# Sixteen-head attention: the divided output multiplied on GpSimd and turned back later, with another opening and another table of places

## The chip, the cores and the metric

The kernel runs on one core of one Trainium2 chip. The metric is the device time of one execution in microseconds (us). Each time given for a kernel is the median of several runs; every profile is of one execution. In the profile the engines are PE (TensorE matmuls), PEld (its weight loads), DVE (VectorE), ACT (ScalarE), POOL (GpSimd) and SP (SyncE, here a queue of DMAs).

## What is computed

A two-layer decoder on x of shape (8, 256, 256), all in float32. Layer 0 adds three results in turn to x: self-attention with 16 heads of width 16, cross-attention of 16 heads over a given context with a key bias and a mask by length, and a feed-forward part in which 8 experts each choose 32 tokens of a batch after a Sinkhorn balancing. Layer 1 adds causal self-attention (16 heads of width 16), a second cross-attention with 16 heads of width 64, and another feed-forward part with routed experts. The change lies in the three attentions with heads of 16:

```python
q, k, v = heads(x @ Wq.T + bq), heads(x @ Wk.T + bk), heads(x @ Wv.T + bv)
q, k = rope(q), rope(k)
attn = softmax(q @ k.T / 4)            # layer 1: causal
out = (attn @ v).merge_heads() @ Wo.T + bo
x = x + out
```

## The kernel before

**Units and steps.** The three attentions are 24 units that run one after the other, one batch each: four times (two self-attentions of layer 0, then two cross-attentions), units 0 to 15, and then eight causal self-attentions of layer 1, units 16 to 23. Each unit has four steps k = 0 to 3. A step is one group of eight heads (c, the half of the width of 256) and one half of the keys (kt); so steps 0 and 1 are group 0, and steps 2 and 3 are group 1.

**A step on the engines.** `scores` (L326) makes the products of keys and queries on PE (`st`, L334), then two exponentials on ACT (`pT`, L345) and, in layer 1, two masking selects on POOL (L350). `values` (L362) multiplies the weights by the values on PE (`o`, L371); the values have a column of ones beside them, so that the sums of the weights come out too. The program issues the scores of the next step ahead of the values of this one. The score tile has one buffer (pool `scp`, L567), so the scores of a step wait until both exponentials of the step before have read it. The output tile `o` has one buffer as well.

**The division.** At the end of a group (odd k) `values` calls `divided_T` (L382): DVE turns `o` in blocks of 32x32 so that queries lie on partitions (`by_q`, L387), takes reciprocals of the sums (`dens`, L389), multiplies (`att`, L391) and turns the result back (`attT`, L397). All four are DVE instructions, one behind the other. There are 48 such groups.

**What stands beside the steps.** The order of every engine is the order in which the code emits instructions (`manual_schedule` over five engines). Work of other units and of the experts is emitted between the steps by a table: `beside(n, k, at, piece)` (L850) puts a piece at step k of unit n, in the order of `at`. Pieces with `at` EARLY (0) come ahead of the values of the step, the others behind them (`run`, L853). A self-attention unit is prepared by such pieces: `stats` and `norm` (L434, L437: layer norm; the power on POOL, L258; the rows on POOL, L262, except in the first two units), `rows` (L444: transposes `tr` on PE), `heads(0)` and `heads(1)` (L452: the product `qk` on PE, three rotary multiplications on DVE, one or two additions on POOL), `joined` (L462: the last addition, on DVE), `vals` (L465), `begin` (L470: the transposes of keys and queries and the masked queries `qm` on ACT). `out(t)` (L486) is the output product of one half of the rows (`ao`) and its addition to x on DVE (L492); it stands in two places, one for each half t. A cross-attention unit's `out` (L552) turns the result back on PE (`oR`) and adds it.

**The experts of layer 0** are the generator `chosen_experts` (L633), one for each pair of batches. It yields 27 times, and four lists, `pieces` (used for the first two pairs), `sooner` and `soonest`, give for each yield its place relative to the unit at which that pair is done. In order the yields are: statistics and norm of the two batches (`xnb`, POOL L262); transposes of each (`tr <- xnb`); the gate product `lg` of each; eight rounds of balancing (`cs`, `rc`, `g`); four rounds of picking the top values, the last of which writes the chosen slots to memory and reads them back by three DMAs (L688 to L694); then one that turns the slots into columns (`cps` on PE, L698, `col`) and makes the first selection matrix (`pick`, POOL L709); and for each batch the gathering product `rps`, the expert product `y` (with `put` on POOL L738 and `ys` on DVE L756), and the scattering product `back`, which is added to x (L765).

**The opening** (the code behind the lists): unit 0 is normed, its heads, values and `joined` are emitted, then unit 1 is normed, unit 0 begins, its first scores are emitted, and only then come the rows and the first heads of unit 1.

**Behind the units** come tables for the second cross-attention (`tables_x`, L807; product `nvw`, L839), that cross-attention (from about 470 us on in the profile) and the last feed-forward part. The change does not touch them.

Of the kernel before, what the change touches and what calls it, by code (L numbers as in the profile page):

```python
# [29 lines left out]
F32 = mybir.dt.float32  # L30
# [4 lines left out]
ALU = mybir.AluOpType  # L35
# [4 lines left out]
P = 128  # L40
B, S, D = 8, 256, 256
# [116 lines left out]
def plain(  # L158
# [121 lines left out]
    def product4(out, lhsT, rhs, start, stop):  # L280
        for h in range(0, P, HP):
            nc.tensor.matmul(  # L282
                out[h : h + HP], lhsT[:, h : h + HP], rhs, start=start, stop=stop, skip_group_check=True
            )
# [31 lines left out]
    class Core:  # L316
# [9 lines left out]
        def scores(self, step):  # L326
# [32 lines left out]
                pTs.append(pT)  # L359
            self.exps[step] = pTs  # L360

        def values(self, step):  # L362


            c, kt, q0 = self.queries(step)
            if kt == 0:
                self.o = op.tile([P, 2, S], F32, tag="o", name="o")
            o, pTs = self.o, self.exps.pop(step)
            for m in range(2):
                for j in range(4):  # L370
                    nc.tensor.matmul(  # L371
                        o[HP * j : HP * j + HP, m, q0:],
                        self.v_pad[:, kt, 8 * c + 2 * j + m, :],
                        pTs[j // 2][:, j % 2, m, : S - q0],
                        start=kt == 0 and m == 0,
                        stop=kt == 1,
                        skip_group_check=True,
                    )
            if kt:
                divided_T(self.attT[:, c, :], o, self.dens[:, c, :])  # L380

    def divided_T(dst, o, r):  # L382


        n = S // HP
        by_q = work.tile([P, 2, n, HP], F32, tag="by_q", name="by_q")
        nc.vector.transpose(by_q.rearrange("p m n w -> p (m n w)"), o.rearrange("p m q -> p (m q)"))  # L387
        r = r.rearrange("p (m n) -> p m n", m=2)
        nc.vector.reciprocal(r, by_q[:, :, :, HD])  # L389
        both = work.tile([P, n, 2, HD], F32, tag="both", name="att")  # L390
        nc.vector.tensor_tensor(  # L391
            both.rearrange("p n m d -> p m n d"),
            by_q[:, :, :, :HD],
            r.unsqueeze(3).to_broadcast([P, 2, n, HD]),
            ALU.mult,
        )
        nc.vector.transpose(dst, both.rearrange("p n m d -> p (n m d)"))  # L397

    def rotary(qk, t, layer, work):
# [26 lines left out]
    class SelfAttention:  # L426
# [10 lines left out]
        def norm(self):  # L437
            self.xn = work.tile([P, 2, D], F32, tag="xn", name="xn")
            for t in range(2):
                self.head = normed(  # L440
                    self.xn[:, t, :], x[:, 2 * self.b + t, :], self.mv, self.rs, t, nc.gpsimd if self.n else nc.vector
                )

        def rows(self):  # L444
# [38 lines left out]
                    xt = x[:, 2 * self.b + t, :]  # L483
                    nc.gpsimd.tensor_tensor(xt, xt, self.bias[1], ALU.add)

        def out(self, t):  # L486
            b, attT = self.b, self.core.attT
            xt = x[:, 2 * b + t, :]
            ps = mm.tile([P, 2 * D], F32, tag="mm", name="ao")[:, :D]
            for c in range(2):  # L490
                product4(ps, attT[:, c, bass.ts(t, P)], self.wo[:, c, :], c == 0, c == 1)
            nc.vector.tensor_tensor(xt, xt, ps, ALU.add)  # L492

# [78 lines left out]
    def turn():  # L574
        for t in range(2):
            qc, qs = rotary(bs[:, :2, :].rearrange("p i d -> p (i d)"), t, 0, work)
            nc.vector.tensor_tensor(turned[:, t, :], qc, qs, ALU.add)
# [272 lines left out]
    def beside(n, k, at, *made):  # L850
        plan.setdefault((n, k), []).append((at, made))

    def run(n, k, early):  # L853
        for at, made in sorted(plan.get((n, k), ()), key=lambda p: p[0]):
            if (at == EARLY) == early:
                for one_made in made:
                    one_made()

    EARLY = 0
    for n, u in enumerate(units):  # L860
        if u.__class__ is SelfAttention:
            u.n = n
            if n in (20, 22):
                beside(n - 2, 0, 80, u.stats)
                beside(n - 2, 1, EARLY, u.norm)
            else:
                beside(n - 3, 2, 80, u.stats)
                beside(n - 3, 3, EARLY, u.norm)
            beside(n - 2, 2, 30, u.rows)
            beside(n - 2, 3, 30, partial(u.heads, 0))  # L870
            beside(n - 1, 0, 30, partial(u.heads, 1))
            beside(n - 1, 1, EARLY, u.joined)
            beside(n - 1, *((2, 30) if u.layer == 0 and n % 4 else (1, 30)), partial(u.vals, 0))
            beside(n - 1, 1, 60, u.begin)
            beside(*((n, 0, 40) if u.layer else (n - 1, 2, 31) if n % 4 else (n - 1, 3, 40)), partial(u.vals, 1))
            beside(n, 3, 80, u.biased)
            for t in range(2):
                beside(n + 1, *((2 + t, 40) if u.layer else (0, 20 + t)), partial(u.out, t))
        else:
            beside(n - 1, 0, 80, u.stats, u.vals)  # L880
            beside(n - 1, 1, EARLY, u.norm)
            beside(n - 1, 1, 60, u.begin)
            beside(n + 1, *((2, 40) if n % 4 == 2 else (0, 20)), u.out)
    beside(0, 2, 40, add_up)
    beside(2, 2, 85, slot_keys)
    beside(3, 2, 50, slot_tables)

    begun = (-1, 2, 80), (0, 0, EARLY), (0, 1, 80)
    start = begun + (
        (0, 2, EARLY), (0, 3, 40), (0, 3, 41), (1, 0, 70), (1, 2, 70),  # L890
        (1, 3, 70), (2, 0, 15), (2, 1, 5), (2, 2, 10), (2, 2, 70), (2, 3, 70), (3, 0, 70), (3, 1, 45),
        (3, 2, 70), (3, 3, 85),
    )
    pieces = start + (
        (4, 1, 85), (4, 2, EARLY), (4, 3, 70), (5, 1, 10), (5, 2, 10), (5, 3, 10), (5, 3, 20), (6, 1, 10), (6, 2, 15),
    )
    sooner = start + (
        (4, 1, 84), (4, 1, 85), (4, 3, 20), (5, 0, 50), (5, 1, 35), (5, 2, 20), (5, 2, 50), (5, 3, 50), (6, 0, 50),
    )
    soonest = begun[:2] + (  # L900
        (0, 0, 80), (0, 1, EARLY), (0, 1, 65), (0, 1, 66), (0, 2, 50), (0, 2, 51),
        (0, 3, 60), (1, 0, 45), (1, 1, 10), (1, 1, 70), (1, 2, 70), (1, 3, 35), (1, 3, 70), (2, 0, 35),
        (2, 0, 70), (2, 1, 85), (2, 2, EARLY), (2, 2, 85),
        (3, 0, 10), (3, 0, 50), (3, 1, 35), (3, 2, 35), (3, 2, 50), (3, 3, 35), (4, 0, 50),
    )
    ex = [chosen_experts(2 * i, 2) for i in range(B // 2)]
    for i, made in enumerate(ex):
        for n, k, at in (pieces, pieces, sooner, soonest)[i]:
            beside(4 * i + 4 + n, k, at, partial(next, made, None))

    for u in units[:2]:
        u.n = 0
        u.stats()
        u.norm()
        if u is units[0]:
            opening = ExitStack()
            opening.enter_context(tc.issue_after(u.head.ins))
            order = ExitStack()
            order.enter_context(tc.manual_schedule(engines=PINNED))
            turn()  # L920
            u.rows()
            u.heads(0)
            u.vals(0)
            u.heads(1)
            u.joined()
            u.vals(1)
            for v in units[:2]:
                v.load()
        else:
            units[0].begin()  # L930
            units[0].core.scores(0)
            u.rows()
            u.heads(0)
            key_tables()
    for n, u in enumerate(units):
        if n == 1:
            expert_tables()
# [22 lines left out]
                wd, ctxs, wproj, wkv_x, wq_x, wout_x, nkrow, nvcol, lns, lnb = weights_x()  # L960
        opening.close()
    order.close()
    for t in range(2):
        units[-1].out(t)
    wn, nvw, hot8 = tables_x(wd, wq_x, wout_x, nkrow, nvcol)
    first.close()
    banks.close()
# [1880 lines left out]
```

## Time and profile before

| what | value |
| --- | --- |
| three runs | 1214.85, 1215.27 and 1216.22 us, median 1215.27 us |
| the profiled execution | 1214.46 us |
| its span, from the first to the last instruction | 1212.7 us |
| PE busy in the span | 1141.0 us (94%) |
| PE busy from 0 to 470 us, the part with the 24 units | 413.04 of 470 us (16.91 of the first 30, 396.13 of the next 440) |
| PE busy from 470 us to the end | 727.99 of 742.70 us |
| DVE, ACT and POOL busy from 30 to 470 us | 288.17, 236.47 and 209.76 of 440 us |

The page lists busy time by engine, then by groups of instructions: line of the code, engine, operation, the tile written and the tiles read, shapes, count; behind a bar the busy time and the mean duration of one in ns; behind the next bar the idle time of that engine just ahead of those instructions and what ended it. In a list in order of time the columns are start (us), duration (us), engine, line, operation, tiles, shape, count, and in brackets the idle time of the engine ahead of it with the instruction that ended it. Matmul durations are pipelined, so a sum of them is more than their busy time.

### The profile page before, as it was taken

The page shows a single profiled execution, that of the slowest core. Times are in us where ns is not written, and L with a number is a line of the kernel's source. Part 1 is how long each engine was busy: PE and PEld are TensorE (multiplying, and loading weights), DVE is VectorE, ACT ScalarE, POOL GpSimd, SP SyncE. Part 2 cuts the span into 40 slices and gives each one's busy share as a digit, 9 for nine tenths or more (in the row PEclk, how much of TensorE's full clock was granted, in tenths as well). Part 3 has the DMA queues.
Part 4 walks back from the last instruction along what each step waited for, and adds up shares of the span by engine and source line. Part 5 has one row for each costly group of instructions (what it writes and reads, how often), then busy time and mean ns, then how long its engine had stood idle before and what let it go on. Part 6 is the DMA issues. An engine that isn't in the chain of part 4 may idle for free.

```text
span 1212.7 us, 31559 instructions
## 1 busy us (share of the span) xinstructions
PE 1141.0 (94%) x13596; PEld 707.9 (58%) x13596; DVE 562.4 (46%) x1564; ACT 447.6 (37%) x696; POOL 417.2 (34%) x482
## 2 busy tenths in 40 slices
PE   5798989998999998999999999999999999999997
PEld 2344435444444445566666676666666486888874
DVE  4455767758775746223332433333335474222113
ACT  2666655656434361223232323232323131222220
POOL 2335344443746741132333323241416105000004
PEclk9999999999999999999999999999999999999999
DMA  7036232050200410010101010101012108599934
GB/s 223 1 127 205 91 117 91 2 171 2 83 2 11 167 71 2 18 37 18 37 19 37 18 37 19 37 19 37 19 37 72 36 2 322 217 399 404 386 123 138
DMA packets 51446, 116.76 MB, mean 96 GB/s; under 512 B 8273, under 2 KB 36417, under 8 KB 46945
## 3 DMA queue, kind: packets, MB, share of 16 engines
q1 hardware_dynamic: 45120, 98.90, 23.9%
q0 software_dynamic: 3456, 12.73, 2.9%
q10 hardware_dynamic: 2720, 3.02, 0.7%
q8 instruction: 109, 1.79, 0.6%
q14 instruction: 41, 0.33, 0.1%
HBM read 104.00 MB, written 27.93 MB: 109 GB/s over the span
## 4 chain that ended last, share of the span: by engine, by line
PE 73%; POOL 8%; DVE 7%; issue 6%; ACT 3%; DMA 2%; SPq 0%; POOLq 0%; ACTq 0%; DVEq 0%
PE h L276 7%; PE k L276 6%; PE v L276 6%; PE wo L276 5%; PE ox L1458 5%; PE stx L1419 4%; PE out L1836 4%; PE out L1653 3%; PE st L334 3%; PE h L1041 3%; PE o L371 3%; PE qk L282 3%; PE q L276 3%; PE tr L291 2%; PE fm L276 2%
## 5 line engine op out<-in xcount | busy, mean ns | idle before, releaser
L345 ACT ACTIVATE pT<-st 128x1024 f32<-128x1024 f32 (+1 forms) x128 | 110.5, 917 | 79.3 <-PE st L334 79.1
L371 PE MATMUL o<-pT,padv 128*32 128x256 f32 (+1 forms) x1536 | 100.4, 372 | 4.3 <-POOL pT L350 4.2
L1425 POOL TENSOR_TENSOR both<-pTx 128x512 f32<-128x512 f32 x64 | 82.1, 1310 | 50.5 <-issue 44.9
L371 PEld LDWEIGHTS o<-pT,padv 128*32 128x32 f32 x1536 | 40.9, 110 | 87.4 <-issue 41.7
L276 PE MATMUL h<-xrT,w 128*64 128x128 f32 (+1 forms) x1936 | 87.3, 250 | 3.1 <-issue 3.1
L276 PEld LDWEIGHTS h<-xrT,w 128*64 128x64 f32 x1936 | 84.7, 137 | 6.1 <-issue 3.9
L258 POOL TENSOR_TENSOR lnrs<-lnve,mhalf 128x2 f32<-128x2 f32 x48 | 35.1, 732 | 153.2 <-DVE lnve L256 141.8
L345 ACT ACTIVATE pT<-st,kbias 128x1024 f32<-128x1024 f32 x64 | 67.8, 1112 | 36.7 <-PE st L334 36.7
L1423 ACT ACTIVATE pTx<-stx 128x1024 f32<-128x1024 f32 x64 | 62.2, 1022 | 41.3 <-PE stx L1419 26.2
L1034 DVE TENSOR_TENSOR midr<-sl,h 128x128 f32<-128x128 f32 x102 | 29.4, 288 | 102.5 <-PE h L276 68.9
L334 PE MATMUL st<-qm,kT 32*128 32x512 f32 (+1 forms) x512 | 68.7, 606 | 5.2 <-ACT pT L345 3.3
L1033 ACT ACTIVATE sl<-h 128x128 f32<-128x128 f32 (+1 forms) x114 | 35.3, 310 | 97.8 <-PE h L276 58.8
L1419 PE MATMUL stx<-qTx,kTx 64*128 64x256 f32 x512 | 64.3, 391 | 2.5 <-ACT pTx L1423 2.5
L282 PE MATMUL qk<-l_wqkv,xnT 128*32 128x512 f32 x512 | 63.9, 616 | 2.2 <-ACT xnT L294 2.2
L1458 PE MATMUL ox<-pTx,vx 128*64 128x256 f32 x512 | 62.3, 385 | 0.0
L1513 POOL TENSOR_TENSOR oT<-oT,rs 128x512 f32<-128x512 f32 x30 | 37.3, 1274 | 66.7 <-DMA rs<-rd 66.7
L258 POOL TENSOR_TENSOR lxrs<-lxve,mhalf 128x2 f32<-128x2 f32 x8 | 5.6, 702 | 154.3 <-DVE sc L1172 123.3
L1419 PEld LDWEIGHTS stx<-qTx,kTx 64*128 64x128 f32 x512 | 46.1, 186 | 20.3 <-ACT pTx L1423 7.2
L276 PE MATMUL wo<-wout_x,oT 128*64 128x256 f32 x512 | 58.0, 379 | 0.0
L350 POOL TENSOR_SCALAR_AFFINE_SELECT pT<-pT 128x512 f32<-128x512 f32 x64 | 42.1, 671 | 39.3 <-ACT pT L345 39.3
L1458 PEld LDWEIGHTS ox<-pTx,vx 128*64 128x64 f32 x512 | 33.9, 136 | 26.4 <-issue 12.1
L1466 DVE COPY oT<-ox 128x512 f32<-128x512 f32 x16 | 11.1, 691 | 81.0 <-PE ox L1458 81.0
(361 smaller groups left out, 2195.1 us busy)
## 6 DMA issues: line engine op xcount, KB each, us to landing
w<-packs SPq DMA_DIRECT2D x22, 1408.0 KB
w<-packs SPq DMA_DIRECT2D x22, 768.0 KB
rs<-rd SPq DMA_DIRECT2D x16, 512.0 KB
packs<-L_ffn_w_eDF SPq DMA_DIRECT2D x8, 704.0 KB
packs<-L_ffn_w_eDF SPq DMA_DIRECT2D x8, 640.0 KB
packs<-L_ffn_w_eFD SPq DMA_DIRECT2D x8, 640.0 KB
ctxT<-ctx_T SPq DMA_DIRECT2D x8, 512.0 KB
wkv_x<-L_xattn_Wkv POOLq DMA_DIRECT2D x1, 4096.0 KB, 14.0
```

The source lines that it names most:

```text
L258: nc.gpsimd.tensor_tensor(rs[:, :n], ve[:, :n], mhalf[:, :n], ALU.pow)
L276: nc.tensor.matmul(out[h], lhsT[:, h], rhs, start=start, stop=stop, skip_group_check=True)
L282: nc.tensor.matmul(out[h : h + HP], lhsT[:, h : h + HP], rhs, start=start, stop=stop, skip_group_check=True)
L334: nc.tensor.matmul(st[:, r, :, :n], self.kT[rows, c, bass.ts(kt, P)], self.qm[rows, :, c, q0:], start=True, stop=True,)
L345: nc.scalar.activation(pT[:, :, :, :n], st[:, 2 * k : 2 * k + 2, :, :n], AF.Exp, scale=self.scale, **kb)
L350: nc.gpsimd.affine_select(out=pT[:, :, :, :P], in_=pT[:, :, :, :P], compare_op=ALU.is_ge, fill=0.0, base=0, pattern=[[0, 2], [0, 2], [1, P ...
L371: nc.tensor.matmul(o[HP * j : HP * j + HP, m, q0:], self.v_pad[:, kt, 8 * c + 2 * j + m, :], pTs[j // 2][:, j % 2, m, : S - q0], start=kt ...
L1419: nc.tensor.matmul(st[:, g, kt, :], kT[rows, c, bass.ts(kt, P)], qT[rows, c, :], start=True, stop=True)
L1423: nc.scalar.activation(pT, st, AF.Exp, scale=scale)
L1425: nc.gpsimd.tensor_tensor(both, pT[:, :, 0, :], pT[:, :, 1, :], ALU.add)
L1458: nc.tensor.matmul(o[XD * g : XD * (g + 1), i, :], v[:, kt, 2 * (c2 + i) + g, :], pT[:, g, kt, :], start=kt == 0, stop=kt == 1, skip_group ...
L1836: nc.tensor.matmul(ps[h], mid[:, i, h], sets[k % len(sets)][1][:, i, :], start=i == 0, stop=i == NFC - 1, skip_group_check=True,)
```

## The change

The diff has five parts.

1. **The division is split.** `divided` keeps the first turn and the reciprocals on DVE, and its multiplication is issued on GpSimd. The turn back is a function of its own (`turned_back`), which a new piece calls at place 84 of steps 1 and 3 of every unit, behind nearly all that stands beside these steps.
2. **The output product of a self-attention unit is one piece**: both halves of the rows into one PSUM tile and one addition to x with 512 elements, at the place where the first half stood (in layer 1 step 2 at 40; the second half stood in step 3).
3. **Other places**: `rows` in layer 1 at 60 instead of 30; a cross-attention's `out` in front of a self-attention at 40 instead of 20; and in the lists of the experts the second yield one step later, the yield with `cps` and `pick` one piece or one step later, the last `back` of the first two pairs one step later, and several in `sooner` and `soonest`.
4. **The norms of units 20 and 22 on DVE** instead of GpSimd.
5. **The opening**: the norm, the rows and the first heads of unit 1 are emitted ahead of the second values, the begin and the first scores of unit 0.

```diff
+        def turn(self, c):
+            turned_back(self.attT[:, c, :], self.both)
...
             if kt:
-                divided_T(self.attT[:, c, :], o, self.dens[:, c, :])
-
-    def divided_T(dst, o, r):
+                self.both = divided(o, self.dens[:, c, :])
+
+    def divided(o, r):
...
-        nc.vector.tensor_tensor(
+        nc.gpsimd.tensor_tensor(
             both.rearrange("p n m d -> p m n d"),
             by_q[:, :, :, :HD],
             r.unsqueeze(3).to_broadcast([P, 2, n, HD]),
             ALU.mult,
         )
+        return both
+
+    def turned_back(dst, both):
         nc.vector.transpose(dst, both.rearrange("p n m d -> p (n m d)"))
...
-                    self.xn[:, t, :], x[:, 2 * self.b + t, :], self.mv, self.rs, t, nc.gpsimd if self.n else nc.vector
+                    self.xn[:, t, :], x[:, 2 * self.b + t, :], self.mv, self.rs, t, nc.gpsimd if self.n not in (0, 1, 20, 22) else nc.vector
...
-        def out(self, t):
-            b, attT = self.b, self.core.attT
-            xt = x[:, 2 * b + t, :]
-            ps = mm.tile([P, 2 * D], F32, tag="mm", name="ao")[:, :D]
-            for c in range(2):
-                product4(ps, attT[:, c, bass.ts(t, P)], self.wo[:, c, :], c == 0, c == 1)
-            nc.vector.tensor_tensor(xt, xt, ps, ALU.add)
+        def out(self):
+            attT, xb = self.core.attT, x[:, 2 * self.b : 2 * self.b + 2, :]
+            ps = mm.tile([P, 2, D], F32, tag="mm", name="ao")
+            for t in range(2):
+                for c in range(2):
+                    product4(ps[:, t, :], attT[:, c, bass.ts(t, P)], self.wo[:, c, :], c == 0, c == 1)
+            nc.vector.tensor_tensor(xb, xb, ps, ALU.add)
...
-            beside(n - 2, 2, 30, u.rows)
+            beside(n - 2, 2, 60 if u.layer else 30, u.rows)
...
-            for t in range(2):
-                beside(n + 1, *((2 + t, 40) if u.layer else (0, 20 + t)), partial(u.out, t))
+            beside(n + 1, *((2, 40) if u.layer else (0, 20)), u.out)
...
-            beside(n + 1, *((2, 40) if n % 4 == 2 else (0, 20)), u.out)
+            beside(n + 1, *((2, 40) if n % 4 == 2 else (0, 40)), u.out)
+    for n, u in enumerate(units):
+        beside(n, 1, 84, partial(turned_again, u, 0))
+        beside(n, 3, 84, partial(turned_again, u, 1))
...
-    begun = (-1, 2, 80), (0, 0, EARLY), (0, 1, 80)
+    begun = (-1, 2, 80), (0, 1, EARLY), (0, 1, 80)
...
-        (4, 1, 85), (4, 2, EARLY), (4, 3, 70), (5, 1, 10), (5, 2, 10), (5, 3, 10), (5, 3, 20), (6, 1, 10), (6, 2, 15),
+        (4, 1, 85), (4, 2, EARLY), (5, 0, 60), (5, 1, 10), (5, 2, 10), (5, 3, 10), (5, 3, 20), (6, 1, 10), (6, 3, 10),
...
-        (4, 1, 84), (4, 1, 85), (4, 3, 20), (5, 0, 50), (5, 1, 35), (5, 2, 20), (5, 2, 50), (5, 3, 50), (6, 0, 50),
+        (4, 1, 84), (4, 1, 85), (5, 0, 20), (5, 0, 50), (5, 1, 35), (5, 2, 50), (5, 3, 10), (5, 3, 60), (6, 0, 50),
...
-    soonest = begun[:2] + (
-        (0, 0, 80), (0, 1, EARLY), (0, 1, 65), (0, 1, 66), (0, 2, 50), (0, 2, 51),
-        (0, 3, 60), (1, 0, 45), (1, 1, 10), (1, 1, 70), (1, 2, 70), (1, 3, 35), (1, 3, 70), (2, 0, 35),
+    soonest = (-1, 2, 80), (0, 0, EARLY), (0, 0, 80), (0, 1, EARLY)
+    soonest += (
+        (0, 2, 35), (0, 2, 36), (0, 3, 10), (0, 3, 50),
+        (1, 0, 10), (1, 0, 70), (1, 1, 35), (1, 1, 70), (1, 2, 70), (1, 3, 35), (1, 3, 70), (2, 0, 35),
         (2, 0, 70), (2, 1, 85), (2, 2, EARLY), (2, 2, 85),
-        (3, 0, 10), (3, 0, 50), (3, 1, 35), (3, 2, 35), (3, 2, 50), (3, 3, 35), (4, 0, 50),
+        (3, 0, 70), (3, 1, 50), (3, 2, 35), (3, 3, 10), (3, 3, 35), (4, 0, 10), (4, 0, 50),
     )
...
-    for u in units[:2]:
-        u.n = 0
-        u.stats()
-        u.norm()
-        if u is units[0]:
...
-            turn()
-            u.rows()
-            u.heads(0)
-            u.vals(0)
-            u.heads(1)
-            u.joined()
-            u.vals(1)
-            for v in units[:2]:
-                v.load()
-        else:
-            units[0].begin()
-            units[0].core.scores(0)
-            u.rows()
-            u.heads(0)
-            key_tables()
+    first_u, second_u = units[:2]
+    first_u.stats()
+    first_u.norm()
...
+    turn()
+    first_u.rows()
+    first_u.heads(0)
+    first_u.vals(0)
+    first_u.heads(1)
+    first_u.joined()
+    second_u.stats()
+    second_u.norm()
+    second_u.rows()
+    first_u.vals(1)
+    first_u.begin()
+    second_u.heads(0)
+    first_u.core.scores(0)
+    key_tables()
...
-    for t in range(2):
-        units[-1].out(t)
+    units[-1].out()
```

`turned_again(u, c)` calls `u.core.turn(c)`. The calls of `load` that the opening loses did nothing for these two units (L430).

## The prediction

> **What bounds the kernel now.** I read the busy times first: PE works 1141.0 of 1212.7 us, and from 470 us to the end 727.99 of 742.70 us. The change touches nothing there, so that part only moves. In the 470 us before it PE works 413.04 us; 57 us are waits, and they are all that a new order can win. The second view lists for what PE waited up to 470 us (total, times, longest, in us):
>
> ```profile
> engine line waited for: us in total, times, longest us
> PE st L334 <- ACT pT L345: 8.5, 8, 1.5
> PE tr L291 <- DVE xn L262: 7.9, 1, 7.9
> PE tr L291 <- DVE qkr L463: 7.8, 7, 1.7
> PE cps L698 <- DMA by_half<-slots: 6.8, 3, 2.9
> PE qpsx L547 <- DVE xnx L262: 4.3, 4, 1.1
> PE o L371 <- POOL pT L350: 4.2, 5, 1.6
> PE back L282 <- DVE ys L756: 3.0, 2, 1.5
> PE tr L291 <- POOL xnb L262: 2.3, 2, 1.5
> ```
>
> No single engine binds; PE stops where a piece stands too early in its queue. The third view, PE in order of time, shows what such a stop costs, and the fourth the clock behind it (busy times by engine, then granted clock, DMA share, GB/s):
>
> ```profile
> 168.34 1.09 PE L291 MATMUL tr<-ident,xnb 128*128 128x128 f32 x8
> 171.60 0.32 PE L698 MATMUL cps<-ident,by_half 4*128 4x4 f32 x2 [2.16 <-DMA by_half<-slots]
> 171.73 2.10 PE L334 MATMUL st<-qm,kT 32*128 32x512 f32 x8
> 173.76 1.68 PE L371 MATMUL o<-pT,padv 128*32 128x256 f32 x16
> ```
> ```profile
> 171.60:175.20 3.60, 3.60 (x26) 1.37 (x30) 0.17 (x1) 1.22 (x2) 2.44 (x3) 0.53 1.03 339
> ```
>
> The reader is to see that `st` elsewhere takes 1.14 us and here 2.10, because after a wait of 2.16 us the clock was 0.53 for 3.6 us. So this wait cost 2.16 + 0.47 x 3.6 = 3.9 us. The one at 246.19 us (2.92 us, then 0.57 for 3.5 us) cost 4.4.
>
> The Trainium skill ("TensorE: Matmul & The Clock Gate", section "What's actually happening") says that the clock halves after an idle window of about 3.4 us. By that rule alone neither wait would have slowed PE, and the forecast would be about 3 us higher; the measured 0.53 decides.
>
> **What goes.** Each place was followed through the compiled order of the changed kernel, with durations of this trace.
> - *`cps` later.* It now stands behind the next scores, values and `ao` (first two pairs) or behind `qk` and `v` (the fourth). First pair: `tr <- xnb` ends at 169.43, the exponentials free the score tile at 169.5, `st` to 170.6, `o` to 171.6, `ao` to 173.4, `cps` (its DMA is long there) and `lg` to 174.1; the next `st` starts at 174.15 instead of 177.38: 3.2 us. Second pair by the same steps 4.4 us. Fourth pair 1.68 us at 375.38. **9.3 us.**
> - *The second yield later.* At 98.02, 161.67 and 235.51 PE waits 0.57, 1.36 and 1.34 us for `qkr` of DVE, which waits for `qc` on POOL, which stands behind two rows of `xnb` (2.42 us). These rows now stand behind `qc`: **3.3 us.** What is next late there, `tr <- qkr`, has its input 0.3 us early by my count.
> - *The last `back` of the first two pairs later.* It waited 1.48 us twice (204.13, 278.80). The step it leaves has 3.0 us of PE work, less than the 3.44 us from one `st` to the next that the exponentials allow (56.04 to 59.48), so 0.4 us of each comes back: **2.1 us.**
> - *`tr <- xnb` of the fourth pair later:* waits of 1.49 and 0.77 us, of which 0.7 comes back, since the last row of `xnb` still ends at 316.7: **1.6 us.**
> - *Units 20 and 22 normed on DVE.* Before, the selects, `xn` on POOL (2.42 us) and the waits around 365 and 411 us cost 1.4 us each. After, DVE waits for the power (`lnrs`, to 362.53) and takes 0.73 us, then `by_q` follows late, and `o` with its single buffer waits 0.6 us: 0.85 twice, **1.7 us.**
>
> Together **18.0 us**.
>
> **What comes.**
> - *The opening.* PE now has unit 1's transposes in front of unit 0's second values. Their input is ready at 21.9 us as before (DVE's order is the same), so PE stands from 16.41 to 21.9, where it had four short waits. From there: transposes, values (at a slow clock, as behind other long waits), `begin`, `qk`, and the first `st` at about 27.9 instead of 21.76 us; but `qk` and the transposes are then done, and the fourth `st` comes at 38.8 instead of 36.85: **2.0 us** lost, from 0 to 4 by how long the clock stays down.
> - *One addition of 512 for two of 256.* Two take 0.42 each, of which the second starts after `ao`; one takes 0.69 (the row of `x<-x,oR`). Where PE then waits for `xnx` (4 times) it waits 0.27 longer: **1.1 us.** The two halves of `ao` in one step of layer 1 are PE work either way; in the last two units, with little else beside them, the chain comes out 0.1 us later.
> - *The product on GpSimd.* The operation isn't in the trace. The nearest rows:
>
> ```profile
> L391 DVE TENSOR_TENSOR att<-by_q,dens 128x256 f32<-128x256 f32 x48 | 22.0, 458 | 1.6
> L484 POOL TENSOR_TENSOR x<-x,offset 128x256 f32<-128x256 f32 x16 | 11.5, 738 | 7.1 <-DVE offset L585 7.1
> L459 POOL TENSOR_TENSOR qkr<-qc,qs 128x512 f32<-128x512 f32 x16 | 20.6, 1284 | 4.3 <-DVE qs L418 3.7
> ```
>
> I take 0.74 us, POOL's own row of as many elements and inputs; the ends are 0.40 (POOL's copy of 128x256 in pieces of 16, L307) and 1.28 (twice the elements). DVE loses 48 x 0.46 = 22 us, POOL gains 48 x 0.74 = 36 us on 210 of 440 us busy. Neither total is a bound; places are. In layer 0 the turn back comes late enough: unit 0's ended at 45.87 and `ao` started at 46.93; product and hand-over add 0.45 us, so 0.6 us is left, and the cover in the other units is like it (0.2 to 1 us). In 28 of 48 groups other DVE work stands between the reciprocals and the turn back; in the other 20 DVE waits about 0.9 us for POOL, with `stats` or an addition behind it. In layer 1 each of 16 products stands in front of the next selects. It starts 1.1 us after `o` ends and takes 0.74; the next first select can start 1.5 us after `o` at the earliest, so the delay is at most 0.35 us, less with filler on PE: 0 to 5.6 us, taken at the middle, **2.8 us.**
> - *Two engines on one memory path.* DVE's `g` (0.19 us) took 1.21 us while POOL added two tensors:
>
> ```profile
> 348.57 1.28 POOL L459 TENSOR_TENSOR qkr<-qc,qs 128x512 f32<-128x512 f32 x1 [1.16 <-DVE qs L418]
> 348.69 1.21 DVE L662 TENSOR_TENSOR g<-g,rc 128x32 f32<-128x32 f32 x1
> ```
>
> With 36 us more of such work on POOL, DVE's additions of two SBUF tensors will be held more often; most have cover of a step. 0 to 4 us, taken at **1.0.**
>
> The Trainium skill ("GPSIMD Engine Reference", section "Engine selection") speaks against this move: two-input elementwise work belongs on VectorE, GpSimd being about twice as slow. The rows agree in kind (738 against 458 ns, 1.6 times); by twice the DVE row the product would take 0.92 us and the layer-1 delay grow by up to 0.18 x 16 = 2.9 us, so about 1207 us.
>
> **The sum.** 18.0 - 2.0 - 1.1 - 0.1 - 2.8 - 1.0 = 11.0 us less. Against the profiled execution's own 1214.46 us (span 1212.7, with 1.76 around it) that is 1203.5; the median of the three runs lies 0.8 us above that execution, so I forecast **1204.3 us**.
>
> **Rivals.**
> - *Wider gain.* DVE, relieved of two instructions in front of the rotary products, hands `qkr` over earlier (waits of 0.93 and 0.43 us at 362 and 408), and the products hide wholly: 11.0 + 2.8 + 1.0 + 1.0, so about 1199.5. For it: the selects had waits of 4.2 us only.
> - *Half is given back.* PE arrives earlier than POOL's `pick` (1.83 us), `put` (1.9) and rows behind it; the five won places turn into waits for these, as the 1.62 us of `o` for the selects at 303 us do now. Half of 18.0 kept: 9.0 - 7.0 = 2 to 5 us, about 1211.
> - *Slower: the selects behind the product.* The product is far slower than my row, or waits long for the reciprocals behind other DVE work, and POOL, which takes its queue in order, holds the masking selects of layer 1. The 16 places must lose 13.8 us (the 11.0 and the 2.8 I already gave) before the change loses, 0.86 us each: a product that ends 1.2 us after the select could start. With 1.2 us of loss each: 1204.3 - 2.8 + 19.2, about 1221. Against it: in the trace POOL's two-input rows hardly vary (716 to 902 ns for L484).
> - *Nothing to measure.* The opening costs its 4 us, the lock its 4, the selects their 5.6, and the wins are 15: about 1215.
>
> **Chances.** The forecast, 1201.5 to 1208: 0.42. Wider gain, 1196 to 1201.5: 0.16. Half, 1208 to 1212.8: 0.19. Nothing, 1212.8 to 1217.7, which is within 0.2%, about what a measurement of this kernel can tell from no change: 0.08. Slower: 0.15. So faster 0.77, same 0.08, slower 0.15. The range is 1197 to 1216; it leaves out the slow rival and the last microsecond of the wide gain.
>
> **What would show it.** In the list of PE's waits: `cps <- by_half` and `back <- ys` gone, `tr <- qkr` down from 7.8 to about 4 us, `tr <- xnb` under 1; one wait of about 5.4 us at 16 us; the clock near 1.0 at 172 and 246 us; `att` on POOL near 740 ns; `o <- pT` from 4.2 to at most 10 us. The start of `fm <- ctxT` (from 471.6 us) should be 11 us earlier, and all behind it unchanged. I am wrong if `o <- pT` grows past 15 us, if `att` takes over 1.2 us, if the opening costs over 4 us, or if new waits for `pick`, `put` or `attT` stand where `cps` and `back` stood.

## The result, and the profile after

The changed kernel takes 1215.33 us (median of 12 runs, 1211.78 to 1217.58), the kernel before 1215.74 us beside it (12 runs, 1208.77 to 1219.43). The ratio is 1.0001, with a 95% interval from 0.9987 to 1.0016: no difference that can be measured, where I forecast 11 us less. The profiled execution took 1217.2 us, so it is one of its longer ones.

The first matmul behind the 24 units (`fm <- ctxT`, first in each fence below from the lists of PE in order of time; changed kernel first, then before) shows that the part that the change touches ended 2.2 us later in this execution, and not 11 us earlier:

```profile
473.78 0.65 PE L276 MATMUL fm<-ctxT,wkv_x 128*64 128x256 f32 x2
```
```profile
471.59 0.65 PE L276 MATMUL fm<-ctxT,wkv_x 128*64 128x256 f32 x2
```

PE's waits from 0 to 470 us in the changed kernel, in the same columns as the prediction's list:

```profile
engine line waited for: us in total, times, longest us
PE tr L291 <- DVE xn L262: 13.0, 2, 7.5
PE st L334 <- ACT pT L345: 10.7, 8, 2.1
PE cs L282 <- DVE g L674: 8.8, 6, 2.7
PE qpsx L553 <- DVE xnx L262: 5.7, 4, 1.5
PE o L374 <- POOL pT L350: 4.3, 6, 1.6
PE ao L282 <- DVE attT L403: 3.2, 1, 3.2
PE o L374 <- DVE by_q L390: 2.6, 3, 1.2
PE tr L291 <- DVE qkr L469: 2.2, 3, 0.9
PE rps L282 <- POOL pick L715: 1.9, 2, 1.7
...
PE tr L291 <- POOL xnb L262: 0.6, 1, 0.6
PE cps L704 <- DMA by_half<-slots: 0.2, 1, 0.2
```

Nearly every wait that I struck out is gone: `cps` from 6.8 to 0.2 us, `tr <- xnb` from 2.3 to 0.6, `tr <- qkr` from 7.8 to 2.2, and `back <- ys` (3.0) is not in the list. The selects, which I feared, cost what they did (4.3 for 4.2). But `cs <- g`, 1.1 us before and no line of my forecast, stands at 8.8 us, and the last `ao <- attT` went from 2.2 to 3.2. The clock is whole where the wait for `cps` stood, as forecast (stretch; busy times of PE, its weight loads, DVE, ACT and POOL, each with its number of instructions; granted clock, DMA share, GB/s):

```profile
171.40:174.80 3.40, 3.40 (x78) 1.85 (x78) 0.53 (x2) 2.04 (x3) 2.29 (x4) 1.00 0.76 240
```

So the question is not whether the gains came, but what took them back.

**A measure for small steps.** The runs of one kernel spread over some 6 us (the changed kernel) to 11 us (the one before). But the order on each engine is fixed, and apart from stretches of half clock (granted clock 0.50 in the profile), and what waits behind them, a step takes the same time to 0.1 us in every kernel whose order there is the same. So besides ratios I compare the start of each step's scores (`st`, in the list of PE in order of time). Changed kernel less before, in us, at the start of units 1, 9, 10, 13, 14, 16, 17, 19 and 23: +1.5, +1.1, -2.4, -1.7, -6.0, -3.7, -6.3, +4.7, +2.7. The two `cps` places show as -3.5 (in unit 9) and -4.3 (in unit 13). Then come losses that I did not forecast: +3.3 in unit 11, +3.3 in unit 15, +11 in units 17 and 18. Steps show one execution, with its own stretches of half clock: the profiled one of the changed kernel has nine up to 470 us, that of before five, and three of the nine lie between units 17 and 19. The changed kernel with `back` put back, whose order is the same there, had none there and took 3.5 us less from the start of unit 17 to that of 20; so part of the 11 us is chance.

### The profile page after: what moved, and what is told of

Read it like the earlier page. It is cut to its first block, busy times and chain, and to the rows that moved or that the text cites. A ratio compares the mean times of both kernels' runs of the same rounds, so it can differ in the third digit from the quotient of the medians.

```text
span 1215.4 us, 31522 instructions
## 1 busy us (share of the span) xinstructions
PE 1143.1 (94%) x13596; PEld 711.9 (59%) x13596; DVE 546.2 (45%) x1504; ACT 447.7 (37%) x696; POOL 440.6 (36%) x526
## 4 chain that ended last, share of the span: by engine, by line
PE 74%; POOL 8%; issue 6%; DVE 5%; ACT 4%; DMA 2%; SPq 0%; POOLq 0%; ACTq 0%; DVEq 0%
PE h L276 7%; PE k L276 5%; PE v L276 5%; PE ox L1466 5%; PE st L334 5%; PE wo L276 4%; PE stx L1427 4%; PE o L374 4%; PE out L1844 4%; PE out L1661 3%; PE qk L282 3%; PE h L1049 3%; PE q L276 3%; ACT pT L345 2%; PE tr L291 2%
## 5 line engine op out<-in xcount | busy, mean ns | idle before, releaser
L276 PEld LDWEIGHTS wo<-wout_x,oT 128*64 128x64 f32 x512 | 36.8, 137 | 18.5
```

The lines of the kernel that those rows point to most:

```text
L276: nc.tensor.matmul(out[h], lhsT[:, h], rhs, start=start, stop=stop, skip_group_check=True)
```

## The experiments

Four batches ran, each on another chip and beside the kernel before, which took 1219.9, 1219.8, 1216.6 and 1220.0 us in them; so each kernel is told by its ratio to before in its own batch. Gains and losses in us are that ratio times before's time, and "by steps" means differences of the starts of `st`.

**First batch: one part at a time.**

```diff
-    begun = (-1, 2, 80), (0, 0, EARLY), (0, 1, 80)
+    begun = (-1, 2, 80), (0, 1, EARLY), (0, 1, 80)
...
-        (4, 1, 85), (4, 2, EARLY), (4, 3, 70), (5, 1, 10), ...
+        (4, 1, 85), (4, 2, EARLY), (5, 0, 60), (5, 1, 10), ...
```

> The kernel before with three numbers of its tables changed: the second yield of the experts one step later for the first three pairs, and the yield with cps and pick one piece of the step later for the first two pairs. Nothing else of the change. Theory A (the gains of the moved places are real, and others of the change gave them back): the two cps places gain 3.5 and 4.3 us as the profile of the changed kernel shows at units 9 and 13, the second yield up to 1.4 us in each of three places, so 7 to 11 us less than before: 1205 to 1209 us. Rival B (the places gain only together with the relief of DVE, since pick, put and the rows behind cps come late in any case): less than 4 us gained, 1212 to 1216 us.

Ratio 0.9924 (0.9902 to 0.9946): 9.3 us less. By steps 3.5 us in unit 9 and 4.3 in unit 13 for `cps`, and 0.1, 0.9 and 0.9 for the second yield of the three pairs, 9.7 in all. At `fm` the difference is 10.0 (461.59 against 471.59): a stretch of half clock more in unit 16 took 1.5 us, and one less near 465 us gave it back. Theory A: two changed entries of the tables ("the three moved numbers" below) win nearly what the whole change was to win.

```diff
-    ... (5, 3, 10), (5, 3, 20), (6, 1, 10), (6, 3, 10),
+    ... (5, 3, 10), (5, 3, 20), (6, 1, 10), (6, 2, 15),
```

> The changed kernel with one place undone: the last back of the first two pairs again in step 2 instead of step 3. Theory A (the wait at back was a wait for DVE's queue; with back gone the next cs stands there and waits longer, 2.69 us at 203 and at 274 us, with half the clock behind it): the two cs waits go, the two back waits of about 1.5 us return, half the clock behind them goes: 2.4 us less at each of the two places, about 1210.5 us against 1215.3 for the changed kernel. Rival B (the moved back was worth the 2.1 us that I forecast, and the loss is elsewhere): 1217 us.

Ratio 0.9951 (0.9937 to 0.9965): 6.0 us less than before, and the changed kernel with `back` moved is level with before (1.0001, in the first comparison). By steps 2.1 us at unit 10 to 12 and 2.6 at 14 to 16: theory A. The list of PE in order of time of the changed kernel shows why:

```profile
198.74 1.07 PE L374 MATMUL o<-pT,padv 128*32 128x256 f32 x16
199.62 0.29 PE L282 MATMUL cs<-g,ones 128*32 128x16 f32 x16
199.85 0.66 PE L291 MATMUL tr<-ident,xn 128*128 128x128 f32 x4
203.19 0.32 PE L282 MATMUL cs<-g,ones 128*32 128x16 f32 x16 [2.69 <-DVE g L674]
203.44 2.09 PE L334 MATMUL st<-qm,memk 32*128 32x512 f32 x8
205.46 1.70 PE L374 MATMUL o<-pT,padv 128*32 128x256 f32 x16
206.99 1.90 PE L282 MATMUL back<-ys,put 128*32 128x256 f32 x32
```

and DVE at the same time:

```profile
199.27 0.48 DVE L745 SCALAR_TENSOR_TENSOR junk<-idx_row,col,later 128x256 f32<-128x256 f32 x1
...
200.88 0.88 DVE L762 TENSOR_SCALAR ys<-y,weight 128x256 f32<-128x256 f32 x2
201.67 0.43 DVE L403 STREAM_TRANSPOSE attT<-att 128x256 f32<-128x256 f32 x1
202.03 0.22 DVE L667 RECIPROCAL rc<-cs 128x16 f32<-128x16 f32 x1
...
202.95 0.19 DVE L674 TENSOR_TENSOR g<-g,rr 128x32 f32<-128x32 f32 x1
```

With `back` put back (same list, this experiment):

```profile
200.75 0.29 PE L282 MATMUL cs<-g,ones 128*32 128x16 f32 x16
202.64 1.93 PE L282 MATMUL back<-ys,put 128*32 128x256 f32 x32 [1.60 <-DVE ys L762]
204.50 0.66 PE L291 MATMUL tr<-ident,xn 128*128 128x128 f32 x4
205.09 0.32 PE L282 MATMUL cs<-g,ones 128*32 128x16 f32 x16
205.34 1.14 PE L334 MATMUL st<-qm,memk 32*128 32x512 f32 x8
```

The reader is to see DVE, not PE. Between the first `cs` and the next one DVE has `junk`, `weight`, `ys`, the turn back and a whole round of balancing, 3.9 us without a pause. The next `cs` needs the last of it. `back` waited 1.6 us in the middle of that chain, and its own 1.93 us covered the rest. Taken out of there, it leaves the chain as long as it was and PE with nothing but 0.66 us of `tr`; it waits 2.69 us at the end of the chain in place of 1.6 in the middle, and does `back` in the next step besides. From one `cs` to the next it is then 3.57 us in place of 4.34, so that step gets 0.8 us shorter; the next gets 3.3 us longer, by `back` itself and by the half clock behind the wait (`st` 2.09 us for 1.14).

```diff
-        nc.gpsimd.tensor_tensor(
+        nc.vector.tensor_tensor(
             both.rearrange("p n m d -> p m n d"),
```

> The changed kernel with the division's product back on DVE, the turn back still at its late place. Theory A (the product is not what the gains were lost to; PE's waits for the selects are 4.3 us in the changed kernel and 4.2 before): within 2 us of the changed kernel, 1213 to 1217 us. Rival B (the hand-over to GpSimd and back, and two engines on one memory path, are what was lost): 4 to 8 us less, 1207 to 1211 us.

Ratio 0.9970 (0.9956 to 0.9984): 3.7 us less, between the two theories. The steps tell more: against the changed kernel nothing changes from unit 1 to unit 16 (0.5 us later at unit 1, 0.7 at unit 16), and 3.8 us are won from the start of unit 16 to that of 23, one stretch of half clock among them. So the product's price is paid in layer 1.

The fourth kernel has the opening of the diff's fifth part, and nothing else of the change.

> The kernel before with the new opening alone. Theory A (the opening costs what the steps of the first units show, 1.5 us at unit 1 and 3.0 at unit 3): 1.5 to 3 us more than before, 1217 to 1219 us. Rival B (cross-attention, where the exponentials set the pace, takes it back): within 1 us of before.

Ratio 1.0019 (1.0006 to 1.0032): 2.3 us more. By steps 2.3 us, from unit 1 unchanged to unit 9; behind it, where the order is that of before, other stretches of half clock make it 2.5 to 4.2. Theory A.

**Second batch: one more part each, on the kernel with the three moved numbers** (0.9924).

The lists `sooner` and `soonest` of the diff:

> The kernel before with the three moved numbers for the first pairs of batches (9.3 us less than before, measured) and the lists of the third and fourth pair of the changed kernel. Theory A (my forecast: the fourth pair's cps 1.7 and tr for xnb 1.6 are gains of their own): about 3.3 us less than without the lists, 12.6 us less than before. Rival B (in layer 1 the new places put other waits where the old ones stood: rps for pick 1.65 us at 326 us and cs for g 1.67 at 352 us of the changed kernel, each with half the clock behind it): 2 to 5 us more than without the lists, 4 to 7 us less than before.

Ratio 0.9906 (0.9881 to 0.9930), 11.5 us less than before; by steps 3.2 us less at unit 23 than without the lists (the ratios' intervals overlap). Theory A by the steps, though new waits for `pick` (1.16 us) and `ys` (1.51) do appear in unit 17.

```diff
-                    ... self.rs, t, nc.gpsimd if self.n else nc.vector
+                    ... self.rs, t, nc.vector if self.n in (0, 20, 22) else nc.gpsimd
```

> The kernel before with the three moved numbers and the norms of units 20 and 22 on DVE. Theory A (my forecast): the waits of tr for xn around 365 and 411 us go, 0.85 us each after what by_q costs: 1.7 us less than without, 11 us less than before. Rival B (o waits 1.17 us for by_q in both places, as in the changed kernel): within 0.7 us of the kernel without it in the places of units 19 to 22.

Ratio 0.9942 (0.9918 to 0.9966), 7.1 us less than before, so no gain on 0.9924; by steps 1.2 us are lost by unit 23. PE's `o` waits 1.17, 0.54 and 1.17 us for `by_q` where `tr` had waited 0.77 twice. Theory A fell, and so did rival B: from unit 19 to 23 2.7 us are lost. Most of it stands at the `cps` of unit 19, which waits 2.52 us in place of 1.68, with half clock behind it.

The split division, its product on GpSimd and the turn back at place 84 of the table, as in the diff's first part:

> The kernel before with the three moved numbers, the division's product on GpSimd and the turn back at its late place. Theory A (my forecast): nothing in layer 0, 2.8 us for the selects and 1.0 for the shared memory path in layer 1, so 3.8 us more than without it, 5.5 us less than before. Rival B (the product and its hand-over are hidden wherever the lists of the experts are the old ones): within 1 us of the kernel without it.

Ratio 1.0008 (0.9984 to 1.0032): the 9.3 us are gone. Both theories missed. By steps layer 0 loses nothing, and units 16 to 19 lose some 11 us: `oR` waits 2.17 us for the turn back at 297 us, `cps` 3.94 us for its DMA at 316 and 2.57 at 375. The trace shows how the late product delays the first of these DMAs (columns as before; SPq issues DMAs):

```profile
303.84 0.26 DVE L392 RECIPROCAL dens<-by_q 128x16 f32<-128x16 f32 x1
304.94 2.42 POOL L262 TENSOR_SCALAR xnb<-x,lnmv,lnrs 128x256 f32<-128x256 f32 x2
307.34 0.61 POOL L394 TENSOR_TENSOR att<-by_q,dens 128x256 f32<-128x256 f32 x1
307.98 0.45 DVE L403 STREAM_TRANSPOSE attT<-att 128x256 f32<-128x256 f32 x1 [3.89 <-POOL att L394]
310.96 0.33 SPq L694 DMA_DIRECT2D slots<-top  x1
```

The product's inputs are ready at 304.1 us, but POOL has two selects and two rows of `xnb` in front of it. DVE stands 3.89 us for the turn back, and the picking of the top values, which ends in those DMAs, stands behind the turn back in DVE's queue. With the three numbers alone the same DMA is issued at 307.03 us. So the price depends on what the lists put in front of the product on POOL and behind the turn back on DVE; no run moved those rows alone.

The output product in one piece, with one addition, as in the diff's second part:

> The kernel before with the three moved numbers and the output product of a self-attention unit in one piece with one addition. Theory A (my forecast): PE waits 0.27 us longer for xnx in four places and 0.1 us at the end, 1.2 us more than without it. Rival B (the four places are hidden behind the exponentials, and one addition less frees DVE): no difference of 0.5 us.

Ratio 1.0023 (0.9998 to 1.0048): 12 us more than without it, against 1.2 in theory A. By steps 0.3 to 0.4 us in each of the four places of layer 0, as forecast, and once more in unit 11; 2.1 us in unit 15, where half clock came up; and 6.6 us in layer 1.

**Third batch: parts of the changed kernel undone in turn, and the merged output product taken apart.**

```diff
-            beside(n + 1, *((2, 40) if u.layer else (0, 20)), u.out)
+            for t in range(2):
+                beside(n + 1, *((2 + t, 40) if u.layer else (0, 20 + t)), partial(u.out, t))
```

> The changed kernel with one part undone: the output product of a self-attention unit again in two halves with an addition each, in the two places of before. The changed kernel takes as long as the one before (ratio 1.0001). Theory A (the merged output product took back most of the gain, as it did by some 9 us on the other base): 5 to 9 us less than before. Rival B (there it was an accident of that base's lists, and the changed kernel's table fits the merged one): within 2 us of before.

Ratio 0.9927 (0.9907 to 0.9947): 8.9 us less than before. Theory A.

The same with the last `back` in step 2:

> The changed kernel with two parts undone: the output product in two halves, and the last back of the first two pairs in step 2 as before. Theory A (the losses are separate and add up: 6 us for back, 5 to 9 for the output product): 11 to 15 us less than before. Rival B (the two share DVE's queue, so that one undone does most of it): 6 to 9 us less than before.

Ratio 0.9925 (0.9906 to 0.9943): 9.1 us less than before, at the upper end of rival B and below theory A. By steps `back` gives 0.5 us at unit 11 and 2.6 at unit 15; the last section shows where the other 2 went.

The same with the product on DVE:

> The changed kernel with three parts undone: the output product, the last back, and the product of the division on DVE again (the turn back at its late place). What is left of the change is the new opening, the lists, the norms on DVE, and the late turn. Theory A (the product costs some 3.5 us in layer 1 with these lists): 3.5 us less than with the product on GpSimd, 14 to 18 us less than before. Rival B (with the output product in two halves the product on GpSimd is hidden): within 1 us of the kernel with two parts undone.

Ratio 0.9861 (0.9839 to 0.9883): 16.9 us less than before (16.6 between the medians). By steps the product's move is worth 0.5 us in layer 0 and 2.8 in layer 1. Theory A. Between the ratios it is 7.8 us, over twice the steps; the two profiled executions are the fastest of the one kernel and the slowest of the other, and which figure is nearer is not settled.

The fourth starts from the three moved numbers:

```diff
-                beside(n + 1, *((2 + t, 40) if u.layer else (0, 20 + t)), partial(u.out, t))
+                beside(n + 1, *((2, 40 + t) if u.layer else (0, 20 + t)), partial(u.out, t))
```

> The kernel before with the three moved numbers, and in layer 1 the second half of the output product moved from step 3 to step 2, straight behind the first; still two tiles and two additions. It parts the place from the single addition. Theory A (the place costs: step 3 and the wait at the end lose the work that filled them, step 2 gets late): most of the 6.6 us that the merged output product lost in layer 1, 4 to 7 us more than with the three numbers alone. Rival B (the single long addition costs, as my forecast had it): within 1 us of the three numbers alone.

Ratio 0.9963 (0.9950 to 0.9976): 4.8 us more than with the three numbers alone; by steps 7.6 us from unit 17 to 23, where the merged one lost 6.7, each with one to two stretches of half clock more than the three numbers alone. Theory A: in layer 1 it is the place, not the long addition. (In layer 0, where the place did not move, the 4 us that the merged one lost are the addition's and the half clock's.) PE in unit 18, first with the half in step 3 (the three numbers alone), then with both halves in step 2:

```profile
338.45 0.29 PE L282 MATMUL cs<-g,ones 128*32 128x16 f32 x16
338.57 1.05 PE L282 MATMUL ao<-l_wo,attT 128*32 128x256 f32 x16
340.33 1.97 PE L727 MATMUL y<-experts,rT 128*32 128x256 f32 x32 [0.71 <-DVE qs L418]
342.40 0.32 PE L282 MATMUL cs<-g,ones 128*32 128x16 f32 x16
342.65 0.71 PE L334 MATMUL st<-qm,kT 32*128 32x256 f32 x8
```
```profile
339.72 0.29 PE L282 MATMUL cs<-g,ones 128*32 128x16 f32 x16
339.84 2.00 PE L727 MATMUL y<-experts,rT 128*32 128x256 f32 x32
343.66 0.32 PE L282 MATMUL cs<-g,ones 128*32 128x16 f32 x16 [1.81 <-DVE g L668]
343.90 0.71 PE L334 MATMUL st<-qm,kT 32*128 32x256 f32 x8
344.55 1.57 PE L371 MATMUL o<-pT,padv 128*32 128x256 f32 x16
```

From one `cs` to the next is 3.95 us with the half in it and 3.94 without. The half of 1.05 us cost nothing in step 3: it lay over DVE's rotary products and its round of balancing. In step 2 it costs its own length, and step 3 takes as long as before; and the wait of 1.81 us that it leaves brings half clock (`o` 1.57 us for 1.07). At the end the last `ao` waits 3.59 us in place of 2.17.

**Fourth batch: what was left, on the version with three parts undone.**

Norms of units 20 and 22 on GpSimd again:

> The version with the output product, the last back and the division's product undone (16.6 us less than before), with the norms of units 20 and 22 on GpSimd again. Theory A (the norms on DVE cost: o waits 1.17 us for by_q where tr waited 0.8 for xn): 1 to 3 us less than that version, 18 to 19 us less than before. Rival B (my forecast: they gain 1.7 us): 1.7 us more.

The opening of before:

> The version with three parts undone (16.6 us less than before), with the opening of before. Theory A (the new opening costs 2.3 us whatever stands behind it): 2 to 3 us less, 18.5 to 19.5 us less than before. Rival B (the merged lists need the new opening's order, or the pace of the exponentials absorbs it): within 1 us.

The turn back straight behind the product:

> The version with three parts undone, with the turn back on DVE straight behind the product, as in before; the table's piece at 84 goes. Theory A (the late turn alone gains or costs nothing to speak of): within 1.5 us of that version. Rival B (the late turn lets the rotary products and the norms go first and is worth 2 to 5 us): 2 to 5 us more.

The product on GpSimd in layer 0 and on DVE in layer 1:

> The version with three parts undone, with the division's product on GpSimd in the sixteen units of layer 0 alone, and on DVE in the eight of layer 1. Theory A (the product is hidden in layer 0, and costs only where GpSimd has the selects and DVE the fourth pair's experts): within 1 us of that version. Rival B (it costs in layer 0 too, through the shared memory path): 2 to 4 us more.

| kernel | ratio to before (interval) | by steps against the version with three parts undone |
| --- | --- | --- |
| three parts undone | 0.9861 (0.9839 to 0.9883) | |
| norms on GpSimd | 0.9865 (0.9839 to 0.9890) | 0.4 us less |
| opening of before | 0.9845 (0.9822 to 0.9867) | 2.6 us less |
| turn back at once | 0.9878 (0.9853 to 0.9902) | 0.3 us more |
| product on GpSimd in layer 0 | 0.9886 (0.9860 to 0.9911) | 0.9 us more in layer 0, then 1.6 less through a stretch of half clock that did not come |

The ratios' intervals overlap; only the steps tell these apart, each in one execution. By them: the norms cost a little (neither theory), the opening 2.6 us (A), the late turn next to nothing (A), the product in layer 0 about 1 us (A at its edge; by the ratios it is 3 us, which would be B, and the profiled execution is the fastest of its five). The version with the opening of before is the fastest of all: 18.9 us less than before, 1202.08 us beside 1219.96.

## Why the prediction was wrong

I forecast 1204.3 us, 11 us less, and gave the case near 1215 a chance of 0.08, for reasons (the opening, the lock, the selects at their upper ends) that did not come about, so it is luck that this rival names the measured time. Term by term, in us, a gain with a minus:

| step of the prediction | forecast | measured | from |
| --- | --- | --- | --- |
| `cps` later, first two pairs | -3.2, -4.4 | -3.5, -4.3 | first kernel, units 9 and 13 |
| second yield later | -3.3 | -1.9 | first kernel |
| fourth pair: `cps`, `tr <- xnb` | -1.7, -1.6 | -3.2 for both lists | lists on the three numbers |
| last `back` later | -2.1 | **+4.7** | `back` undone |
| units 20 and 22 normed on DVE | -1.7 | +0.4 | norms on GpSimd again |
| opening | +2.0 | +2.3 | opening alone |
| one output product (places, one addition, end) | +1.2 | **+8.7** | output in halves, start of `fm` |
| product on GpSimd and the shared memory path | +2.8, +1.0 | +3.8 | product on DVE again |

- **Two steps of the prediction failed in kind: "the last `back` of the first two pairs later" and "the two halves of `ao` in one step of layer 1 are PE work either way".** Both ask only how long the moved piece itself waits or works. Both pieces stood in a stretch that DVE sets: between two rounds of balancing PE has to fill 3.9 us of DVE's chain. What leaves such a stretch shortens it little (0.8 us for `back`, nothing for the half of `ao`), and it costs most of its length where it goes. I counted a wait as lost time of the piece that it stands at; it was time of DVE's queue, and the next piece that needs that queue inherited it. And I counted half clock behind the waits that go, but none behind waits that come: the later `back` costs 0.5 us at the one place where the difference holds no half clock, and 2.1 to 2.6 where it does.
- **The opening, the lists and `cps` were right** in mechanism and within about 1 us in size.
- **The product's path was wrong in layer 1.** It took 0.62 us on GpSimd (row below), less than my 0.74 and within my ends, and PE's waits for the selects, which I priced at 2.8 us, did not grow (4.3 for 4.2). I gave DVE's wait for POOL 0.9 us in 20 groups. In the changed kernel the turn back waits for the product 28 times, 34.9 us in all: 0.6 to 0.8 us each in layer 0, and up to 3.9 in layer 1, where the product stands behind rows of a norm, selects or `pick` in POOL's queue. Its price of 3.8 us met my sum with the changed kernel's lists (3.7 us by ratio in the first batch, 3.3 by steps and 7.8 by ratios in the third), and with the old ones it was some 10 us. The Trainium skill's figure that I weighed against it ("GPSIMD Engine Reference", section "Engine selection", about twice as slow) is too high for this shape: 617 against 458 ns is 1.35 times.

```profile
L394 POOL TENSOR_TENSOR att<-by_q,dens 128x256 f32<-128x256 f32 x48 | 29.6, 617 | 43.0 <-DVE dens L392 43.0
```

- **The second yield** was mis-sized: 1.9 for 3.3 us. Each of the three places gave about 0.45 us less than the wait that I struck out there (0.1, 0.9 and 0.9 for 0.57, 1.36 and 1.34).
- **The norms**: I took 0.6 us for the wait of `o` for `by_q`, and it is 1.17. On the three numbers alone they lost 1.2 us by steps.
- **The terms do not add up simply.** Measured one at a time they come to 7.0 us slower, while the profile shows 2.2 and the medians none. Two that share a wait are counted twice: `back` undone alone gives 6.0 us, the output product alone 8.9, both together 9.1.
- Of the signs that I named, those on single waits came true; `att` on POOL was 617 ns for 740, and the sum, the start of `fm`, failed. My last one ("new waits for `pick`, `put` or `attT` stand where `cps` and `back` stood") had the right idea and mostly the wrong names: `rps` does wait 1.65 us for `pick` at 326 us, but the large one is the next `cs`, 8.8 us.

How the price of the mistake splits between DVE's late chain itself and the half clock behind its waits is settled only for `back`, by the figures above; for the output product it stays open, and it depends on the execution.

## What to carry to other kernels

Before moving a piece away from a wait, follow the engine that it waits for up to the next piece that needs that engine: a piece is worth moving away from a wait of the kind "PE waits 1.5 us for DVE" only if PE does not need a later result of that same chain soon after. A piece that fits inside a chain set by another engine is nearly free there, and can cost its whole length elsewhere. And a change of many parts that comes out level is worth taking apart: here some parts won 13 us and the others lost them, and the version without the largest losses is 18.9 us faster than before (14.2 us at the start of `fm` in the two profiled executions).

## What the runs showed of the hardware

**Half clock comes in stretches of 3.41 us on a fixed grid.** In the changed kernel five of them begin at 203.4, 275.1, 326.3, 353.6 and 367.2 us: 21, 15, 8 and 4 times 3.41 us apart. The profiled execution has nine such stretches up to 470 us (two of them in the opening), that of before five; each costs PE up to 1.7 us of work, half its length. Over the twelve runs of the changed kernel the mean granted clock goes from 0.994 (1211.8 us) to 0.987 (1217.6). By my estimate 0.007 of 1215 us is 8.5 us, five such stretches, so their number can make up the whole spread of runs. A wait does not always bring one. In the version with the output in halves, `cs` waits 2.29 us both at 200.58 and at 269.65 (stretches of that execution's grid, columns as above):

```profile
196.18:199.59 3.41, 2.11 (x40) 1.16 (x36) 3.16 (x13) 3.13 (x5) 1.75 (x2) 1.00 0.46 153
199.59:203.01 3.42, 2.43 (x45) 1.21 (x49) 2.64 (x13) 0.91 (x1) 0.00 (x0) 1.00 0.96 273
267.86:271.27 3.41, 1.62 (x32) 0.75 (x36) 2.69 (x13) 0.63 (x3) 0.00 (x0) 1.00 0.00 0
271.27:274.69 3.42, 3.42 (x40) 1.75 (x36) 2.06 (x7) 2.02 (x2) 2.03 (x3) 0.50 0.00 0
```

The same wait, once with the whole clock behind it and once with half. The first is parted between two stretches of the grid, in which PE works 2.11 and 2.43 us; the second lies mostly in one, in which it works 1.62. That is why `back` undone gave 0.5 us in one place and 2.6 in the other there. Laid on each execution's own grid, the 18 profiles (from 30 us on, up to 8 us before the end) show the same: of the stretches at whole clock, all 29 in which PE was busy less than 0.42 were followed by half clock, 28 of the 72 between 0.42 and 0.56, and none of the 5979 above. In the changed kernel the wait of 2.69 us brought it both times; PE was busy 0.71 of the 3.4 us ahead of the first:

```profile
199.90:203.30 3.40, 0.71 (x19) 0.47 (x19) 2.93 (x12) 1.63 (x3) 0.64 (x1) 1.00 0.85 231
203.40:206.80 3.40, 3.40 (x39) 1.18 (x30) 2.19 (x10) 1.14 (x2) 0.70 (x1) 0.50 1.00 371
```

The Trainium skill ("TensorE: Matmul & The Clock Gate", section "What's actually happening") says that the monitor's window is 3413 ns long and runs freely, so that where it falls differs from run to run. The stretches of 3.41 us, their grid and the two equal waits agree with that. It gives an idle window as the condition for half clock; here windows with 0.71 and 1.62 us of work were enough.

**The chips differ at the very end.** From the start of `fm` to the end the kernels of the first, second and fourth batch took 743.0 to 746.5 us, those of the third and of the first comparison 741.0 to 741.6, with the same instructions. The difference lies behind the last matmul, where the last results are stored: 6.4 to 7.0 us in the third batch and the first comparison, 7.9 to 9.7 in the others. From `fm` to the end of the last matmul it is 734.2 to 736.1 us everywhere, and 736.9 and 737.1 in the two executions with a stretch of half clock there. So only ratios within a batch were compared.
